# Two graph layers with attention on one core: order of batch 1, of the adjacency transposes, of the folds and of the ending

## The chip, the cores and the metric

The kernel runs on one core of one Trainium2 chip. The metric is the device time of one execution in microseconds (us). The kernel before takes 2221.71 us (median of three runs, 2218.53 to 2224.95). Its profiled execution spans 2219.8 us from the first to the last instruction; all times inside the kernel count from that start. A core has a matrix engine (TensorE, PE in the profile), a vector engine (VectorE, DVE), an activation engine (ScalarE, ACT), GpSimd (POOL) and SyncE (SP), which here issues nearly all transfers (DMA). Each engine takes its instructions in the order in which the program gives them.

## The reference, cut to what matters

Sixteen batches of x (1024 nodes by 256 channels) share one adjacency matrix of 1024 by 1024. Two layers follow each other, each added to its input and normalized over the channels:

```python
# layer 0
c_adj = x.mean(-1)                                  # one mean per node
A = abs(abs(sigmoid(c_adj_i - c_adj_j) - 0.5) - 0.5) * 2
Wg = adj * (A + A.T) * 0.5
q = relu((x.T @ Wg) * para)                         # the query graph, 4 heads of 64
k, v = split(x @ kv_w)
x1 = layernorm(x + softmax(q k.T * scale) v)
# layer 1
h1 = relu(x1 @ w1_loop + adj @ (x1 @ w1_neigh) + b1)
h2 = relu(h1 @ w2_loop + adj @ (h1 @ w2_neigh) + b2)
out = layernorm(x1 + (x1 + h2) * 0.5)
```

## The kernel before

Everything is float32, and a float32 matmul is recorded as two instructions. `run` (line 810) writes the order of all work out by hand; nothing reorders it (`tc.manual_schedule`). The loop over b (line 861) does the attention of batch b in four units of a head pair and half of the nodes (`UNITS`), and lays other batches' work into the gaps between the units: the convolutions of earlier batches, the queries of batch b+1.

`Attention.scores(u)` (line 505) makes eight score tiles of 128 by 1024 in PSUM; ACT exponentiates each into a tile `pr`, and DVE adds the eight up into `acc` (line 522), turns the sum (`accB`, line 524) and reduces it to `den_part` (line 526). `outputs(u)` (line 528) multiplies the `pr` by the values. `add(u)` (line 539) folds `den_part` over partitions with one matmul (line 545), then DVE divides, adds the result to the blocked residual `xB`, and reduces it to `sums` (line 556).

A mean or a variance over 256 channels is taken from a blocked layout with two tiles of 128 channels. DVE reduces each tile to 32 columns (`part` or `sums`, two blocks of columns), and `fold_sums` (line 252) adds the partitions of both with two matmuls into one PSUM tile. There are three such folds for most batches: `means` (line 260) for the query graph of the next batch, `BlockedNorm.mean` (line 305) and `BlockedNorm.variance` (line 319).

The query graph of a batch needs the weighted adjacency, tile by tile: ACT makes the likeness (line 381), DVE multiplies it by a row block of adj (`times_adj`, line 387), PE multiplies (`step`). Batches 0 and 1 use the plain `Queries` (line 364), later ones `FastQueries` (line 407), which saves one product in eight by sums of blocks (`left`, `right`).

The convolutions need adj transposed. After batch 0's attention the branch at line 946 loads adj once more in a blocked layout (`adj_blocked`, line 204) and DVE turns it (`turn_adj`, line 840) into three constant half tiles and two row tiles `rows01`. For later batches the products of two batches are joined with block sums of the adjacency (`Joined`, line 737); these sums are made once, by `adj_sums` (line 189), in batch 1's second gap (`gap1`, line 889, the branch without `both`), and parked in DRAM. That gap also has the first product of batch 0's convolution, `c1.first(rows01)` (line 644), and `weigh_first` (line 881), the first weighted tiles of batch 2's query graph. Each `Joined.run` (line 772) runs seven products in an order of its own and calls other work between them.

SBUF for tiles of 128 by 1024 comes from one pool of 23 buffers (`row_tile`, line 99). A new tile waits until the last reader of the buffer that it gets is done, a DMA to DRAM included.

After the loop, from line 1007 on, the last two batches' convolutions are joined, and batch 15's second half is done alone: `second` (line 676) with 32 matmul records, then `ending` (line 715), which takes the output in four quarters of 256 nodes. Each quarter has its products (`outer`, line 686), its residual (line 692), its statistics (line 273), a power on POOL for the deviation (line 282), and then `leave`, which normalizes on DVE (line 288) and writes. Batch 14's output is normalized on DVE just before (`finish`, line 711).

Of the kernel before, what the change touches and what calls it, by code (L numbers as in the profile page):

```python
# [10 lines left out]
F32 = mybir.dt.float32  # L11
I32 = mybir.dt.int32
AF = mybir.ActivationFunctionType
ALU = mybir.AluOpType
# [4 lines left out]
def kernel(  # L19
# [31 lines left out]
    nc = tc.nc  # L51

    B, N, C = x.shape
    P = 128
    NT = N // P
    NC = C // P
# [5 lines left out]
    TJ = FB // P  # L62
# [8 lines left out]
    NB = N // S  # L71

    LIFT = 32.0
    UNITS = [(pair, j) for pair in range(NC) for j in range(NJ)]
# [5 lines left out]
    small = ctx.enter_context(tc.tile_pool(name="small", bufs=4))  # L80
# [105 lines left out]
    def adj_block(i, j, k, rows01):  # L186
        return of_rows(rows01, k) if (i, j) == (0, 1) else half_adj[i, j][:, k, :]
# [56 lines left out]
    def prepare(blocked, name):  # L244

        xT = channel_major(blocked, f"xT_{name}")
        part = small.tile([P, NC, NB], F32, tag="part", name=f"part_{name}", bufs=2)
        for cc in range(NC):
            nc.vector.tensor_reduce(part[:, cc, :], blocked[cc].rearrange("p (bn r) -> p bn r", r=S), AX.X, ALU.add)
        return xT, part  # L250

    def fold_sums(part, name):

        pm = bank_psum(f"{name}_ps")
        for cc in range(NC):
            nc.tensor.matmul(pm[:, 0:NB], fold.rearrange("p a k -> p (a k)"), part[:, cc, :],
                             start=(cc == 0), stop=(cc == NC - 1))
        return pm[:, 0:NB]

    def means(part, name):  # L260

# [34 lines left out]
    def by_node(t):  # L296
        return t.rearrange("p (bn r) -> p bn r", r=S)

    class BlockedNorm:
# [12 lines left out]
        def squares(self):  # L312
            self.part = small.tile([P, NC, NB], F32, tag="part", name=f"sq_part_{self.name}", bufs=2)
            for cc in range(NC):
                sq = row_tile(f"sq_{self.name}_{cc}")
                nc.scalar.activation(sq, self.xB[cc], AF.Square)  # L316
                nc.vector.tensor_reduce(self.part[:, cc, :], by_node(sq), AX.X, ALU.add)

        def variance(self):
            self.rstd = small.tile([P, NB], F32, tag="rstd1", name=f"rstd1_{self.name}", bufs=2)  # L320
# [171 lines left out]
    class Attention:  # L492
# [46 lines left out]
        def add(self, u):  # L539

            b, (pair, j) = self.b, UNITS[u]
            half = FB // S
            pd = bank_psum(f"den_ps_{b}_{u}")
            den = pd[:, 0:2 * half]
            nc.tensor.matmul(den, fold.rearrange("p a k -> p (a k)"), self.part.pop(u), start=True, stop=True)
            rden = small.tile([P, half], F32, tag="rden", name=f"rden_{b}_{u}", bufs=2)
            for s in range(2):
                rows = slice(s * HD, (s + 1) * HD)
                nc.vector.reciprocal(rden[rows, :], den[rows, ts(s, half)])
            nc.vector.tensor_tensor(den_min, den_min, den, ALU.min)  # L550
            nc.vector.tensor_tensor(den_max, den_max, den, ALU.max)
            o = by_node(self.o.pop(u))
            nc.vector.tensor_mul(o, o, rden.unsqueeze(2).to_broadcast([P, half, S]))
            dst = by_node(self.xB[pair][:, ts(j, FB)])
            nc.vector.tensor_add(dst, dst, o)
            nc.vector.tensor_reduce(self.sums[:, pair, ts(j, half)], dst, AX.X, ALU.add)

    def safe_attention(b, xb, qT, kT, v):

# [54 lines left out]
    class GraphConv:  # L614
# [58 lines left out]
                nc.tensor.transpose(pt[:, ts(i, P)], self.h1T[:, ts(j * TJ + i, P)], ident)  # L673
            nc.scalar.copy(self.h1[:, ts(j, FB)], pt)

        def second(self, rows01):

            self.uT = row_tile(f"uT_{self.b}")
            for j in range(NJ):
                pu = half_psum(f"u_ps_{self.b}_{j}")  # L680
                for mt in range(NT):
                    nc.tensor.matmul(pu, self.h1[:, ts(mt, P)], adj_block(mt // TJ, j, mt % TJ, rows01),  # L682
                                     start=(mt == 0), stop=(mt == NT - 1))
                nc.scalar.copy(self.uT[:, ts(j, FB)], pu)

        def outer(self, g, per, p2):
# [25 lines left out]
            normalize(self.mv, self.rstd, self.x)  # L712
            nc.sync.dma_start(out=dst.rearrange("(t p) c -> p t c", p=P), in_=self.x)

        def ending(self, dst):

            per = FB // C
            parts = []

            def leave(g, mv, rstd):  # L720
                rows = self.x[:, g * per:(g + 1) * per, :]
                normalize(mv, rstd, rows, per)
                nc.sync.dma_start(out=dst[g * per * P:(g + 1) * per * P, :].rearrange("(t p) c -> p t c", p=P), in_=rows)

            for g in range(NT // per):
                p2 = (bank_psum if g % 2 else half_psum)(f"h2e_ps_{g}")
                self.outer(g, per, p2)
                self.residual(g, per, p2)
                mv = small.tile([P, per, 2], F32, tag="mv_e", name=f"mv_e_{g}", bufs=2)
                statistics(mv, self.x[:, g * per:(g + 1) * per, :], range(per), f"e{g}")  # L730
                rstd = reciprocal_deviation(mv, f"e{g}", EPS2, per)
                if parts:
                    leave(*parts.pop())
                parts.append((g, mv, rstd))
            leave(*parts.pop())

    class Joined:
# [34 lines left out]
        def run(self, between=None):  # L772
            c1, c2, b = self.c1, self.c2, self.b
            between = between or {}

            def turn_to(n):
                for f in between.get(n, ()):
                    f()

            first, third, second = (half_psum(f"hu_ps_{b}_{i}") for i in range(3))  # L780
            s12, s34 = (row_tile(f"snap_{b}_{k}") for k in range(2))
            p1, u1, u3, p7 = s12[:, 0:FB], s12[:, FB:N], s34[:, 0:FB], s34[:, FB:N]
            self.product(1, first, start=True)
            nc.scalar.copy(p1, first)
            turn_to(1)
            c1.loop(third, 0, start=True)
            self.product(2, third)
            nc.vector.tensor_add(p1, p1, third)
            turn_to(2)
            self.product(6, first, again=True)  # L790
            nc.scalar.copy(u1, first)
            c1.relu(0, p1)
            turn_to(6)
            self.product(7, second, start=True)
            nc.scalar.copy(p7, second)
            turn_to(7)
            self.product(5, first, again=True)
            nc.scalar.copy(u3, first)
            turn_to(5)
            self.product(4, second, again=True)  # L800
            c2.uT = row_tile(f"uT_{c2.b}")
            nc.vector.tensor_add(c2.uT[:, 0:FB], u1, second)
            nc.gpsimd.tensor_add(c2.uT[:, FB:N], u3, p7)
            turn_to(4)
            c1.loop(first, 1, again=True)
            self.product(3, first, again=True)
            c1.relu(1, first)
            turn_to(3)

    def run():  # L810
# [27 lines left out]
        rows01 = []  # L838
# [22 lines left out]
        for b in range(B):  # L861
# [19 lines left out]
            def weigh_first():  # L881
                q.times_adj(0)
                q.times_adj(TJ)
                q.right(0)

            def next_means():
                q.c_row, q.c_col = means(ready["part"], str(b + 1))

            def gap1():
                for t in (0, TJ):  # L890
                    q.load(t)
                if both:
                    both.fetch(1, 4)
                    both.run({1: (lambda: q.left(nc.gpsimd),),
                              2: (lambda: att.add(1), next_means),
                              6: (lambda: q.likeness(0), lambda: c3 and c3.moments()),
                              7: (lambda: q.likeness(TJ),),
                              5: (weigh_first,),
                              4: (lambda: c3 and c3.finish(out[b - 3]),),
                              3: (c1.turn_blocks,)})  # L900
                else:
                    q.left(nc.gpsimd)
                    next_means()
                    for t in (0, TJ):
                        q.likeness(t)
                    c1.first(rows01)
                    att.add(1)
                    weigh_first()
                    c1.turn_blocks()
                    store("01", rows01)  # L910
                    adj_sums(rows01)

            def gap2():
                if both:
# [31 lines left out]
            if more and not c1:  # L946
# [9 lines left out]
                q.times_adj(4)  # L956
                q.step(1)
                att.add(3)
                turn_adj(range(4))
                for mt in range(4, NT):  # L960
                    tiles[mt] = adj_blocked(mt)
                q.times_adj(5)
# [12 lines left out]
                qT = q.end()  # L975
                norm.scale()
                norm.spread()
                turn_adj(range(4, NT))
                kT, v = keys(b + 1, xT), values(b + 1, xT)
            elif more:  # L980
                xT = ready["xT"]
# [36 lines left out]
        c2.last()  # L1018
        c1.turn(1)
        c2.moments()  # L1020
        c1.second(rows01)
        c2.finish(out[B - 2])
        c1.ending(out[B - 1])

    with tc.manual_schedule():
        run()
# [66 lines left out]
```

## Time and profile before

| engine | busy us | share of the span |
|---|---|---|
| PE | 2183.0 | 98% |
| DVE | 1858.4 | 84% |
| ACT | 965.4 | 43% |
| POOL | 328.5 | 15% |

The table is part 1 of the page. The mean granted TensorE clock is 0.995 of full speed. DMA moves 258.61 MB, a mean of 117 GB/s. A line of the timeline has the start and the time from the first start to the last end of a run of like instructions, the engine, the source line, what is written from what, the number of records, and in brackets the idle time ahead of it with what ended it. In the chain of waits a matmul's time counts only until the next one starts, so that it is shorter than the same matmul in the timeline. Where batches 2 to 14 run, PE has no idle gaps worth the name: batch 2's first scores start at 290.81 and batch 3's at 425.76 us.

### The profile page before, as it was taken

The numbers are of one execution on the slowest core, as the hardware profiler recorded it, in microseconds if no ns is written. First come the engines' busy times: TensorE is split into PE (matmuls) and PEld (weight loads), VectorE is DVE, ScalarE is ACT, GpSimd is POOL, SyncE is SP. The second block draws the span as 40 slices with busy tenths as digits, with TensorE's granted clock in tenths as the row PEclk, the third lists the DMA queues.
The fourth block names the chain that finished last, engine by engine and source line by source line (L and its number), as shares of the span: only waits on it lengthen the run. The fifth ranks groups of instructions, "written<-read, shape, count | busy, mean of one in ns | idle before, by whom it ended". The sixth has DMA issues, their size and how long they took to land.

```text
span 2219.8 us, 22852 instructions
## 1 busy us (share of the span) xinstructions
PE 2183.0 (98%) x8190; PEld 1044.3 (47%) x8190; DVE 1858.4 (84%) x2413; ACT 965.4 (43%) x1056; POOL 328.5 (15%) x177
## 2 busy tenths in 40 slices
PE   8997999999999999999999999999999999999997
PEld 4343354544445444454444444445454544544454
DVE  4987987899888988889889788898889888888965
ACT  4733545443454344544435454434544445444410
POOL 1000030120302103021030210303012020210021
PEclk9999999999999999999999999999999999999999
DMA  8292562452726436363364634637254273633342
GB/s 192 86 138 51 153 180 67 75 172 57 180 86 110 137 60 178 98 150 104 59 176 89 171 95 72 167 65 180 86 89 158 57 180 92 139 113 62 108 144 85
DMA packets 586360, 258.61 MB, mean 117 GB/s; under 512 B 488064, under 2 KB 552448, under 8 KB 586240
## 3 DMA queue, kind: packets, MB, share of 16 engines
q1 hardware_dynamic: 585968, 256.56, 47.8%
q8 instruction: 66, 1.08, 0.2%
q14 instruction: 54, 0.44, 0.1%
q10 hardware_dynamic: 272, 0.52, 0.1%
HBM read 210.90 MB, written 46.14 MB: 116 GB/s over the span
## 4 chain that ended last, share of the span: by engine, by line
PE 90%; DVE 5%; SPq 2%; DMA 1%; POOL 1%; issue 0%; ACT 0%; DVEq 0%; POOLq 0%
PE s L513 19%; PE av L533 18%; PE hu_ps L769 15%; PE g_ps L470 15%; PE k_ps L347 4%; PE v_ps L359 4%; PE h_ps L689 2%; PE h_ps L690 2%; PE t_ps L629 2%; PE hu_ps L636 2%; DVE acc L522 2%; PE g_ps L397 2%; SPq L108 1%; PE u_ps L682 1%; PE h_ps L649 1%; DMA xB<-in_x_dram 1%
## 5 line engine op out<-in xcount | busy, mean ns | idle before, releaser
L516 ACT ACTIVATE pr<-s 128x1024 f32<-128x1024 f32 x512 | 477.0, 1051 | 194.7 <-PE s L513 180.7
L522 DVE TENSOR_TENSOR acc<-acc,pr 128x1024 f32<-128x1024 f32 x384 | 493.2, 1284 | 40.7 <-DVE acc L522 0.5
L513 PE MATMUL s<-qT,kT 64*128 64x512 f32 x2048 | 461.1, 600 | 12.4 <-ACT pr L516 11.7
L533 PE MATMUL av<-pr,v 128*64 128x512 f32 x2048 | 453.6, 595 | 0.0
L513 PEld LDWEIGHTS s<-qT,kT 64*128 64x128 f32 x2048 | 191.9, 187 | 250.3 <-ACT pr L516 127.4
L533 PEld LDWEIGHTS av<-pr,v 128*64 128x64 f32 x2048 | 141.3, 137 | 300.1 <-issue 290.3
L323 POOL TENSOR_TENSOR rstd<-rstd,neg_half 128x32 f32<-128x32 f32 x16 | 87.0, 5441 | 1169.1 <-DVE rstd L321 1169.1
L383 ACT ACTIVATE wg<-c_row,c_col 128x1024 f32<-128x1024 f32 x128 | 147.1, 1149 | 81.9 <-DVE accB L524 49.0
L389 DVE SCALAR_TENSOR_TENSOR wg<-wg,adj 128x1024 f32<-128x1024 f32 x128 | 149.7, 1209 | 10.7 <-ACT wg L384 10.7
L769 PE MATMUL hu_ps<-adj,R 128*128 128x512 f32 x360 | 158.4, 596 | 0.0
L384 ACT ACTIVATE wg<-wg 128x1024 f32<-128x1024 f32 x128 | 135.4, 1058 | 4.1
L316 ACT ACTIVATE sq<-xB_a 128x1024 f32<-128x1024 f32 x32 | 33.8, 1057 | 196.3 <-DVE xB_a L310 182.8
L347 PE MATMUL k_ps<-xT,kvw_sb 128*128 128x512 f32 x256 | 117.1, 601 | 0.0
L470 PE MATMUL g_ps<-wg,S 128*128 128x512 f32 x224 | 116.7, 603 | 0.0
L470 PE MATMUL g_ps<-T,S 128*128 128x512 f32 x224 | 114.4, 592 | 0.0
L359 PE MATMUL v_ps<-kvw_sb,xT 128*128 128x256 f32 x512 | 113.1, 379 | 0.0
L769 PE MATMUL hu_ps<-adjT,t 128*128 128x512 f32 x240 | 109.5, 599 | 2.2 <-ACT t L632 2.2
L328 DVE TENSOR_TENSOR xB_a<-xB_a,rstd 128x1024 f32<-128x1024 f32 x32 | 38.8, 1254 | 84.4 <-POOL rstd L323 84.4
L470 PE MATMUL g_ps<-wg,x 128*128 128x512 f32 x224 | 109.0, 599 | 0.0
L520 DVE TENSOR_TENSOR acc<-pr,pr 128x1024 f32<-128x1024 f32 x64 | 78.0, 1218 | 34.6 <-ACT pr L516 34.6
L359 PEld LDWEIGHTS v_ps<-kvw_sb,xT 128*128 128x128 f32 x512 | 97.3, 190 | 20.0 <-issue 7.7
L769 PEld LDWEIGHTS hu_ps<-adj,R 128*128 128x128 f32 x360 | 67.3, 190 | 78.9 <-issue 78.0
(162 smaller groups left out, 2727.3 us busy)
## 6 DMA issues: line engine op xcount, KB each, us to landing
adj<-in_adj_dram SPq DMA_DIRECT2D x128, 512.0 KB, 4.5
adj<-adjT SPq DMA_DIRECT2D x120, 512.0 KB, 8.2
xB_a<-in_x_dram SPq DMA_DIRECT2D x128, 128.0 KB, 4.1
x1d<-xB_a SPq DMA_DIRECT2D x128, 128.0 KB, 3.4
x<-x1d SPq DMA_DIRECT2D x16, 1024.0 KB, 6.6
xB<-in_x_dram SPq DMA_DIRECT2D x120, 128.0 KB, 4.6
x<-in_x_dram SPq DMA_DIRECT2D x15, 1024.0 KB, 7.2
out_dram<-x SPq DMA_DIRECT2D x15, 1024.0 KB, 4.6
```

Source lines behind the costliest of these rows:

```text
L323: nc.gpsimd.tensor_tensor(self.rstd, self.rstd, neg_half, ALU.pow)
L347: nc.tensor.matmul(pk[:, ts(j, FB)], kvw_sb[:, cc, ts(kb, P)], xT[:, cc, ts(j, FB)], start=(cc == 0), stop=(cc == NC - 1))
L359: nc.tensor.matmul(pv[:, ts(i, C)], xT[:, cc, ts(g * per + i, P)], kvw_sb[:, cc, C:2 * C], start=(cc == 0), stop=(cc == NC - 1))
L383: nc.scalar.activation(wg, self.c_row, AF.Abs, bias=self.c_col[:, t:t + 1], scale=-1.0)
L384: nc.scalar.activation(wg, wg, AF.Tanh, scale=-0.5)
L389: nc.vector.scalar_tensor_tensor(wg, wg, 1.0, self.adj.pop(t), op0=ALU.add, op1=ALU.mult)
L470: nc.tensor.matmul(self.p[n], x_n[:, k, :], w_n, start=(k == 0), stop=(k == TJ - 1))
L513: nc.tensor.matmul(ps[:, ts(s, FB)], self.kT[rows, pair, ts(mt, P)], self.qT[rows, pair, ts(j, FB)], start=True, stop=True)
L516: nc.scalar.activation(pr, ps, AF.Exp)
L522: nc.vector.tensor_add(acc, acc, pr)
L533: nc.tensor.matmul(pav[s * HD:(s + 1) * HD, :], self.v[:, mt, pair * P + s * HD:pair * P + (s + 1) * HD], self.pr[mt][:, ts(s, FB)], start ...
L769: nc.tensor.matmul(dst, self.x[n][:, k, :], half_adj[w][:, k, :] if w else of_rows(rows, k), start=(start and k == 0), stop=(k == TJ - 1), ...
```

## The change

The change has five parts. (1) In batch 1's second gap, the adding of unit 1, the likeness tiles, the block sums of the adjacency and the first weighted tiles come ahead of batch 0's first convolution product instead of behind it. (2) The first eight transposes of the adjacency, which lay inside batch 0's query-graph steps for batch 1, go behind it, so that all sixteen follow each other. (3) DVE joins the two column blocks of a partial sum with one addition of 128 by 32, so that a fold has one matmul instead of two. (4) In `Joined.run` the loop product (`c1.loop`) comes ahead of product 1 instead of between products 1 and 2. (5) At the end, the quarters 0 and 1 are done inside batch 15's second product, as soon as their half is ready, and batch 14's last normalization goes from DVE to ACT, in the form scale times x plus a shift. The purpose is fewer waits and fewer instructions on TensorE and a shorter end behind its last matmul.

```diff
@@ -247,15 +247,17 @@
         part = small.tile([P, NC, NB], F32, tag="part", name=f"part_{name}", bufs=2)
         for cc in range(NC):
             nc.vector.tensor_reduce(part[:, cc, :], blocked[cc].rearrange("p (bn r) -> p bn r", r=S), AX.X, ALU.add)
+        join(part)
         return xT, part
 
     def fold_sums(part, name):
 
         pm = bank_psum(f"{name}_ps")
-        for cc in range(NC):
-            nc.tensor.matmul(pm[:, 0:NB], fold.rearrange("p a k -> p (a k)"), part[:, cc, :],
-                             start=(cc == 0), stop=(cc == NC - 1))
+        nc.tensor.matmul(pm[:, 0:NB], fold.rearrange("p a k -> p (a k)"), part[:, 0, :], start=True, stop=True)
         return pm[:, 0:NB]
+
+    def join(part):
+        nc.vector.tensor_add(part[:, 0, :], part[:, 0, :], part[:, 1, :])
 
     def means(part, name):
 
@@ -315,6 +317,7 @@
                 sq = row_tile(f"sq_{self.name}_{cc}")
                 nc.scalar.activation(sq, self.xB[cc], AF.Square)
                 nc.vector.tensor_reduce(self.part[:, cc, :], by_node(sq), AX.X, ALU.add)
+            join(self.part)
 
         def variance(self):
             self.rstd = small.tile([P, NB], F32, tag="rstd1", name=f"rstd1_{self.name}", bufs=2)
@@ -554,6 +557,8 @@
             dst = by_node(self.xB[pair][:, ts(j, FB)])
             nc.vector.tensor_add(dst, dst, o)
             nc.vector.tensor_reduce(self.sums[:, pair, ts(j, half)], dst, AX.X, ALU.add)
+            if u == len(UNITS) - 1:
+                join(self.sums)
 
     def safe_attention(b, xb, qT, kT, v):
 
@@ -673,14 +678,20 @@
                 nc.tensor.transpose(pt[:, ts(i, P)], self.h1T[:, ts(j * TJ + i, P)], ident)
             nc.scalar.copy(self.h1[:, ts(j, FB)], pt)
 
-        def second(self, rows01):
+        def neighbours(self, j, pu, mts, rows01):
+            for mt in mts:
+                nc.tensor.matmul(pu, self.h1[:, ts(mt, P)], adj_block(mt // TJ, j, mt % TJ, rows01),
+                                 start=(mt == 0), stop=(mt == NT - 1))
+
+        def second(self, rows01, between=None):
 
             self.uT = row_tile(f"uT_{self.b}")
             for j in range(NJ):
                 pu = half_psum(f"u_ps_{self.b}_{j}")
-                for mt in range(NT):
-                    nc.tensor.matmul(pu, self.h1[:, ts(mt, P)], adj_block(mt // TJ, j, mt % TJ, rows01),
-                                     start=(mt == 0), stop=(mt == NT - 1))
+                self.neighbours(j, pu, range(TJ), rows01)
+                if j and between:
+                    between()
+                self.neighbours(j, pu, range(TJ, NT), rows01)
                 nc.scalar.copy(self.uT[:, ts(j, FB)], pu)
 
         def outer(self, g, per, p2):
@@ -712,7 +723,16 @@
             normalize(self.mv, self.rstd, self.x)
             nc.sync.dma_start(out=dst.rearrange("(t p) c -> p t c", p=P), in_=self.x)
 
-        def ending(self, dst):
+        def finish_aside(self, dst):
+
+            shift = small.tile([P, NT], F32, tag="shift", name=f"shift_{self.b}", bufs=1)
+            nc.vector.scalar_tensor_tensor(shift, self.mv[:, :, 0], -1.0, self.rstd, op0=ALU.mult, op1=ALU.mult)
+            for t in range(NT):
+                nc.scalar.activation(self.x[:, t, :], self.x[:, t, :], AF.Identity, bias=shift[:, t:t + 1],
+                                     scale=self.rstd[:, t:t + 1])
+            nc.sync.dma_start(out=dst.rearrange("(t p) c -> p t c", p=P), in_=self.x)
+
+        def ending(self, dst, rows01, aside):
 
             per = FB // C
             parts = []
@@ -722,7 +742,7 @@
                 normalize(mv, rstd, rows, per)
                 nc.sync.dma_start(out=dst[g * per * P:(g + 1) * per * P, :].rearrange("(t p) c -> p t c", p=P), in_=rows)
 
-            for g in range(NT // per):
+            def quarter(g):
                 p2 = (bank_psum if g % 2 else half_psum)(f"h2e_ps_{g}")
                 self.outer(g, per, p2)
                 self.residual(g, per, p2)
@@ -732,6 +752,10 @@
                 if parts:
                     leave(*parts.pop())
                 parts.append((g, mv, rstd))
+
+            self.second(rows01, lambda: (aside(), quarter(0), quarter(1)))
+            quarter(2)
+            quarter(3)
             leave(*parts.pop())
 
     class Joined:
@@ -780,10 +804,10 @@
             first, third, second = (half_psum(f"hu_ps_{b}_{i}") for i in range(3))
             s12, s34 = (row_tile(f"snap_{b}_{k}") for k in range(2))
             p1, u1, u3, p7 = s12[:, 0:FB], s12[:, FB:N], s34[:, 0:FB], s34[:, FB:N]
+            c1.loop(third, 0, start=True)
             self.product(1, first, start=True)
             nc.scalar.copy(p1, first)
             turn_to(1)
-            c1.loop(third, 0, start=True)
             self.product(2, third)
             nc.vector.tensor_add(p1, p1, third)
             turn_to(2)
@@ -901,14 +925,14 @@
                 else:
                     q.left(nc.gpsimd)
                     next_means()
+                    att.add(1)
                     for t in (0, TJ):
                         q.likeness(t)
-                    c1.first(rows01)
-                    att.add(1)
-                    weigh_first()
-                    c1.turn_blocks()
                     store("01", rows01)
                     adj_sums(rows01)
+                    weigh_first()
+                    c1.first(rows01)
+                    c1.turn_blocks()
 
             def gap2():
                 if both:
@@ -956,7 +980,6 @@
                 q.times_adj(4)
                 q.step(1)
                 att.add(3)
-                turn_adj(range(4))
                 for mt in range(4, NT):
                     tiles[mt] = adj_blocked(mt)
                 q.times_adj(5)
@@ -975,7 +998,7 @@
                 qT = q.end()
                 norm.scale()
                 norm.spread()
-                turn_adj(range(4, NT))
+                turn_adj(range(NT))
                 kT, v = keys(b + 1, xT), values(b + 1, xT)
             elif more:
                 xT = ready["xT"]
@@ -1018,9 +1041,7 @@
         c2.last()
         c1.turn(1)
         c2.moments()
-        c1.second(rows01)
-        c2.finish(out[B - 2])
-        c1.ending(out[B - 1])
+        c1.ending(out[B - 1], rows01, lambda: c2.finish_aside(out[B - 2]))
 
     with tc.manual_schedule():
         run()
```

## The prediction

> **What bounds the kernel now.** I read the page's part 1 first, then the waits of PE, then the timelines of PE and DVE around the longest of these waits, then the chain of waits in a quiet batch, and last the DVE timeline of the end.
>
> ```profile
> PE 2183.0 (98%) x8190; PEld 1044.3 (47%) x8190; DVE 1858.4 (84%) x2413; ACT 965.4 (43%) x1056; POOL 328.5 (15%) x177
> PE s L513 <- ACT pr L516: 11.7, 2, 10.1
> ...
> PE hu_ps L769 <- ACT t L632: 2.2, 2, 1.1
> PE den_ps L545 <- DVE den_part L526: 1.9, 1, 1.9
> PE g_ps L397 <- DVE wg L389: 1.8, 1, 1.8
> ```
>
> PE has work in 98% of the span and follows itself almost everywhere. So an instruction taken off PE shortens the kernel by its own time, and besides that only the waits (us in total, times, longest) and the work behind the last matmul can be won. DVE, 84% busy, matters where it makes PE wait. That is batch 1; here is PE's timeline:
>
> ```profile
> 187.60 0.63 PE L256 MATMUL mean_ps<-part,fold 128*128 128x32 f32 x4
> ...
> 205.31 0.30 PE L545 MATMUL den_ps<-den_part,fold 128*128 128x32 f32 x2
> 205.55 3.70 PE L513 MATMUL s<-qT,kT 64*128 64x512 f32 x16
> 210.84 1.13 PE L513 MATMUL s<-qT,kT 64*128 64x512 f32 x4 [1.59 <-ACT pr L516]
> 222.08 4.58 PE L513 MATMUL s<-qT,kT 64*128 64x512 f32 x12 [10.11 <-ACT pr L516]
> 226.58 7.09 PE L533 MATMUL av<-pr,v 128*64 128x512 f32 x32
> 235.62 0.46 PE L545 MATMUL den_ps<-den_part,fold 128*128 128x32 f32 x2 [1.95 <-DVE den_part L526]
> 236.01 8.73 PE L513 MATMUL s<-qT,kT 64*128 64x512 f32 x32
> ```
>
> and DVE's over the same gap:
>
> ```profile
> 194.73 0.19 DVE L270 TENSOR_REDUCE c_col<-own 128x8 f32<-128x32 f32 x1
> 205.66 0.52 DVE L549 RECIPROCAL rden<-den_ps 64x16 f32<-64x16 f32 x2 [10.73 <-PE den_ps L545]
> ```
>
> DVE sits idle for 10.73 us because unit 1's fold stands on PE behind the whole convolution product. Then it works without a gap until 235.6, and PE waits in its turn.
>
> A fold's price stands in the chain of waits of batch 3's query graph (start, us, what):
>
> ```profile
> 396.35 0.14 PE den_ps L545 x2
> ...
> 402.58 0.36 PE sum_ps L256 x4
> ```
>
> One matmul takes 0.14 us and two take 0.36, so the second is worth 0.22. At the end DVE runs alone (its timeline):
>
> ```profile
> 2201.68 0.69 DVE L694 TENSOR_TENSOR z<-h2e_ps,b_sb 128x512 f32<-128x512 f32 x1 [4.47 <-PE h2e_ps L690]
> ...
> 2204.41 0.69 DVE L694 TENSOR_TENSOR z<-h2e_ps,b_sb 128x512 f32<-128x512 f32 x1
> ...
> 2211.16 0.68 DVE L694 TENSOR_TENSOR z<-h2e_ps,b_sb 128x512 f32<-128x512 f32 x1
> ...
> 2214.88 0.73 DVE L288 TENSOR_SCALAR x<-x,mv_e,rstd_e 128x256 f32<-128x256 f32 x2 [0.27 <-POOL rstd_e L282]
> ```
>
> Four quarters follow each other, 2.73 us each up to the next z, plus 0.73 for a quarter's normalization.
>
> [...] in the windows view the granted clock is 0.50 from 218 to 222, inside the 10.11 us gap, and 0.50 again from 236 to 238, behind a gap of only 1.95; behind gaps of 1.10 and 1.81 it stays 1.00. [...] the page shows one load, at the start. [...]
>
> **The change part by part.**
>
> *Folds.* Batches 1 to 15 have three folds, batch 0 two: 47. One lies in batch 1's stalled stretch and is counted there, so 46 x 0.22 = 10.1 us come off PE. The joins add 47 small DVE additions; min on 128x32 (L550) takes 0.19 us and starts 0.10 before the next instruction, so I take 0.1 us each. A join lies ahead of its fold, so I looked at the slack in batch 3: the last `sums` are done at 400.6 and the fold comes at 402.4; `sq_part` is done at 410.4, its fold comes at 414.9. Behind the join on DVE stands `pair(3)`; its first part ends at 402.8 for a matmul at 405.4. Slack of 1.8 us and more covers 0.1 to 0.2, so the joins cost nothing. Bounds: 8 to 10.5.
>
> *Transposes.* Eight transposes (3.67 + 1.31 us with a DMA wait, 124.14 to 129.4) go from ahead of `times_adj(5)` to the end. PE's 1.81 us wait was for that multiplication, which now ends near 125.4, ahead of its matmul at 128.5: 1.8 us won. The sixteen then take 16 x 0.6 = 9.7 us. The scale must wait for POOL's power (5.45 us, L323), whose variance comes 2 us earlier; scale and spread end near 146.4, the transposes at 156.2. Batch 1's first addition of `acc` is due at 158.66 - 2.2 = 156.4. It just fits; a miss is taken up by the 2.60 us for which DVE waits next (L549 at 173.62). Bounds: 1 to 2.
>
> *Batch 1.* PE now has unit 1's fold right behind the mean's, at 188.1, but `den_part` is done by DVE only at 192.65. That is a new wait of 4.6 us, and behind it on PE stand the 17.2 us of the convolution and all of unit 2. DVE: c_col done at 194.9, the adding 2.8, eight block sums 9.3 (214.55 to 223.84), weights 4.9 (208.46 to 213.38), h1B 1.15: free at 213.1. PE: 192.9 + 17.2 = 210.1, or 211.8 with a clock dip [...]. I take the dip, since 4.6 us is longer than a gap that showed one. Scores start at 211.8; the first addition of `acc` comes 3.15 us later (as from 425.76 to 428.91 in batch 3), at 214.95; DVE takes 11.7 us for eight tiles and their reduction (223.84 to 235.58): `den_part` is done at 226.7. PE's outputs end at 211.8 + 7.07 + 7.02 = 225.9, so 0.8 of the wait of 1.95 is left. Unit 3's scores take 7.07 at full clock and end at 234.0 instead of 244.67: 10.7 us won. Without the dip it is 12.2. The buffers: ACT's `pr` waited for h1B's store (10.2 us by ACT's waits) since 18 buffers were taken in between; now the sums are written from 197.7 to 207.0 and their stores (1.25 us apart before, each landing in 5.6) start earlier, so they should be free when the first `pr` asks at 212. Bounds: 7.5 to 12.5.
>
> *Loop product first.* In the gaps of the loop PE is busy either way: nothing. In the two runs of the end, PE waits 1.10 us each for t's copy; 1.72 us of loop products now cover it: 2.2 us.
>
> *End.* Quarters 0 and 1 (3.46 us of PE) move ahead of the last 16 matmul records, so the product ends at 2199.91 + 3.46 = 2203.37. Quarter 2 needs the copy that ACT then makes (0.58 and some hand-over: 0.65), a new wait on PE with only the last two quarters behind it. Its products end at 2205.8; DVE: 2.73 + 0.73 + 2.73 + 0.73, then the power (0.72) in part behind it: the last normalization starts at 2212.85 instead of 2214.88. 2.0 us won. [...] Bounds: 0.5 to 2.5.
>
> Sum: 10.1 + 1.8 + 10.7 + 2.2 + 2.0 = 26.8. 2221.7 - 26.8 = 2194.9.
>
> **The rivals.**
>
> *The wait moves (0.24).* PE's new 4.6 us, a clock dip [...] and late buffers leave 7.5 in batch 1; the joins push some folds (8.5); the end gives 0.5, the rest 3. 19.5 us: 2202. For it: the dip behind only 1.95 us. Against it: DVE, which sets unit 2's end, has no other idle time to gain or lose there.
>
> *No dip at all (0.14).* 12.2 in batch 1 and the upper bounds (10.5, 2, 2.2, 2.5): 29.4 us, 2192.3. For it: the gap is one of DVE's order, and 1.81 us left the clock alone. [...]
>
> *DVE becomes the bound (0.03), slower.* If each join waited in line and `sums` reached PE late by 2 us in all 16 batches, 32 us would be lost against 26.8 won: about 2227. Against it: the slack of 1.8 us and DVE's 361 us of idle time. I also leave 0.02 for folds and waits that only just cancel.
>
> **How the numbers follow.** The forecast as worked out has 0.57, and its time is 2194.9. The range takes in the first rival and the second, with the spread of a measurement of about 3 us on the lower side of the estimate: 2188 to 2203. Faster by more than 0.3% means below 2215: 0.95; within it 0.02; slower 0.03.
>
> **What would show it.** Right: L256 with 94 records instead of 188; PE's waits for `pr` and for t gone; one of about 4.6 us for `den_part` near 186 in their place; no wait for wg at L389; batches 0.66 us closer (134.95 to 134.3); the last L288 ending about 10 us behind the last product of L682 instead of 15.7. Wrong: a wait for `sums` or `part` at L256 in every batch, DVE late for batch 1's `acc`, or ACT held by buffers under unit 2.

## The result, and the profile after

The changed kernel takes 2200.87 us (median, 2200.6 to 2201.87) against 2221.61 for the kernel before: a ratio of 0.9907, 95% interval 0.989 to 0.9924. 20.7 us are won where 26.8 were forecast. The time lies inside the forecast's range; 6 us are missing.

Part 1 of the changed kernel's page, busy time and instructions of each engine:

```profile
PE 2172.8 (99%) x8096; PEld 1032.4 (47%) x8096; DVE 1864.0 (85%) x2453; ACT 969.3 (44%) x1064; POOL 328.1 (15%) x177
```

PE is still the engine that is nearly always busy. Its waits in the changed kernel (us in total, times, longest):

```profile
PE den_ps L548 <- DVE o L540: 5.6, 1, 5.6
...
PE k_ps L350 <- DVE U L483: 2.8, 13, 0.5
PE den_ps L548 <- DVE den_part L529: 0.8, 1, 0.8
...
PE h2e_ps L700 <- ACT uT L695: 0.7, 1, 0.7
```

The waits for `pr`, for t and for wg are gone, as forecast. The wait of 5.6 for unit 1's fold and of 0.7 for the copy at the end are the two that the forecast named. The line with U was not forecast: in 13 of the 14 query graphs of batches 2 to 15, the keys (the matmuls into `k_ps`) now wait for the DVE addition U (L483), the first of the additions that end a query graph.

Batch 1, PE's timeline:

```profile
184.31 0.41 PE L256 MATMUL mean_ps<-part,fold 128*128 128x32 f32 x2
190.28 0.64 PE L548 MATMUL den_ps<-den_part,fold 128*128 128x32 f32 x2 [5.56 <-DVE o L540]
190.73 3.74 PE L641 MATMUL h_ps<-x1T,w1l_sb 128*128 128x512 f32 x4
...
209.84 7.14 PE L516 MATMUL s<-qT,kT 64*128 64x512 f32 x32
216.91 7.09 PE L536 MATMUL av<-pr,v 128*64 128x512 f32 x32
224.78 0.41 PE L548 MATMUL den_ps<-den_part,fold 128*128 128x32 f32 x2 [0.78 <-DVE den_part L529]
225.12 7.14 PE L516 MATMUL s<-qT,kT 64*128 64x512 f32 x32
```

The four records of the loop product behind the wait take 3.74 us, in the kernel before 1.96:

```profile
188.06 1.96 PE L636 MATMUL h_ps<-x1T,w1l_sb 128*128 128x512 f32 x4
```

That is the clock dip of the forecast: in the windows view the granted clock is 0.50 from 187.5 to 194.3. Unit 2 has no gap inside any more.

The end, DVE's timeline, first lines of quarters 0, 2 and 3 and the last normalization:

```profile
2178.71 0.69 DVE L705 TENSOR_TENSOR z<-h2e_ps,b_sb 128x512 f32<-128x512 f32 x1 [3.54 <-PE h2e_ps L701]
...
2186.54 0.69 DVE L705 TENSOR_TENSOR z<-h2e_ps,b_sb 128x512 f32<-128x512 f32 x1 [1.55 <-PE h2e_ps L701]
...
2189.92 0.69 DVE L705 TENSOR_TENSOR z<-h2e_ps,b_sb 128x512 f32<-128x512 f32 x1
...
2193.65 0.74 DVE L290 TENSOR_SCALAR x<-x,mv_e,rstd_e 128x256 f32<-128x256 f32 x2 [0.26 <-POOL rstd_e L284]
```

Only two quarters are left behind the last product.

To see where the time went, I cut the span of each profiled execution at five matmuls that all kernels have. "Periods" is the sum of the 13 intervals from batch 2's first keys to batch 15's.

| stage, us | before | after | won |
|---|---|---|---|
| start to batch 1's first keys | 141.65 | 138.36 | 3.29 |
| to batch 2's first keys | 134.84 | 125.71 | 9.13 |
| the 13 periods | 1756.25 | 1752.35 | 3.90 |
| to batch 15's first `t_ps` | 71.67 | 71.55 | 0.12 |
| to batch 15's second product (first `u_ps`) | 81.60 | 78.51 | 3.09 |
| to the end | 33.79 | 32.32 | 1.47 |

13 periods with three folds of 0.22 each should have given 8.6 us; they gave 3.9. The second row was forecast at 11.1 (10.7 and two folds) and gave 9.1. These two rows hold the missing 6 us. The chain of waits at batch 3's keys shows why; here it is in the changed kernel (start, us, what):

```profile
395.56 2.37 DVE sq_part L319 x2
397.92 0.02 issue
397.95 0.19 DVE sq_part L260
398.14 0.61 DVE U L483
398.75 0.04 issue
398.79 3.70 PE k_ps L350 x8
402.49 0.14 PE sum_ps L256 x2
```

The fold is down to 0.14, but the chain now runs through DVE: squares, join, U, and then PE. `k_ps` takes the PSUM tile whose second half U reads last. Here are U, PE's last query-graph matmuls and the keys, from the timelines of both kernels. Under them is a line of the waits of each for PEld, the loading of a matmul's weights, which the profile lists apart from PE. Before:

```profile
410.35 0.68 DVE L480 TENSOR_TENSOR U<-P,g_ps 128x512 f32<-128x512 f32 x1
410.59 1.02 PE L470 MATMUL g_ps<-wg,S 128*128 128x512 f32 x2
411.44 3.60 PE L347 MATMUL k_ps<-xT,kvw_sb 128*128 128x512 f32 x8
...
PEld k_ps L347 <- DVE U L480: 4.5, 13, 0.6
```

After:

```profile
398.06 0.68 DVE L483 TENSOR_TENSOR U<-P,g_ps 128x512 f32<-128x512 f32 x1
397.60 1.02 PE L473 MATMUL g_ps<-wg,S 128*128 128x512 f32 x2
398.79 3.70 PE L350 MATMUL k_ps<-xT,kvw_sb 128*128 128x512 f32 x8 [0.17 <-DVE U L483]
...
PEld k_ps L350 <- DVE U L483: 14.5, 14, 1.3
```

Before, U ended at 411.03 and the keys started at 411.44, 0.85 us behind the start of the last query-graph matmuls. After, U ends at 398.74; the keys start 0.05 behind that and 1.19 behind those matmuls. So they are 0.34 us late, and the eight records take 0.10 longer. This 0.44 is more than the bracket's 0.17: the wait is counted from the listed end of the matmul ahead, and before, the keys started 0.17 ahead of that end.

### The profile page after: what moved, and what is told of

It reads as the page before. It is cut to its first block, busy times and chain, and to the rows that moved or that the text cites. A ratio compares the mean times of both kernels' runs of the same rounds, so it can differ in the third digit from the quotient of the medians.

```text
span 2198.8 us, 22720 instructions
## 1 busy us (share of the span) xinstructions
PE 2172.8 (99%) x8096; PEld 1032.4 (47%) x8096; DVE 1864.0 (85%) x2453; ACT 969.3 (44%) x1064; POOL 328.1 (15%) x177
## 4 chain that ended last, share of the span: by engine, by line
PE 72%; DVE 24%; issue 2%; ACT 1%; DMA 0%; DVEq 0%; SPq 0%; POOLq 0%; ACTq 0%; POOL 0%
PE hu_ps L793 16%; PE s L516 15%; PE av L536 15%; DVE acc L525 6%; PE k_ps L350 5%; PE v_ps L362 5%; PE t_ps L634 3%; PE h_ps L700 2%; PE hu_ps L641 2%; PE g_ps L400 2%; PE h_ps L701 2%; DVE wg L392 2%; DVE sq_part L319 1%; DVE wg L446 1%; DVE T L445 1%
```

## The experiments

All medians are of several timed runs; the kernel before took 2221.4 to 2222.0 beside them. The changed kernel was not timed again beside them, so differences from it of less than about 1 us say little.

**Folds alone.** The kernel before with `join` and the single matmul in `fold_sums`, nothing else:

```diff
+        nc.tensor.matmul(pm[:, 0:NB], fold.rearrange("p a k -> p (a k)"), part[:, 0, :], start=True, stop=True)
-        for cc in range(NC):
-            nc.tensor.matmul(... part[:, cc, :], start=(cc == 0), stop=(cc == NC - 1))
+    join(part) / join(self.part) / join(self.sums)
```

> Only the joined sums and single folds are put into the kernel before. Theory A (in every query graph of batches 2 to 15 the keys' first PSUM buffer is now awaited from the DVE addition U, because DVE is 0.23 us later by two joins and PE 0.44 us earlier by two folds, against a slack of 0.41): each of 14 batches keeps only 0.23 of its 0.66 us, so 47 x 0.22 - 14 x 0.43 = 4.3 us are won, about 2217.3. Theory B (the folds pay in full and the gain is lost elsewhere): 10.3 us won, about 2211.3.

Measured 2216.81 (2214.21 to 2218.93), ratio 0.9976, interval 0.9968 to 0.9983: 5.2 us won. Its trace has the same wait:

```profile
PE k_ps L350 <- DVE U L483: 2.4, 13, 0.5
```

So half of the folds' gain is lost with a wait that this part alone brings. That is near theory A's 4.3 us and far from theory B's 10.3. The sizes in theory A do not give its own result, though: 0.23 later and 0.44 earlier against a slack of 0.41 make 0.26 a batch, and its 0.43 was read from the periods. The true sizes come with the idle joins below.

**Two matmuls for a fold again, no joins.** The reverse of it, in the changed kernel:

```diff
-        nc.tensor.matmul(... part[:, 0, :], start=True, stop=True)
+        for cc in range(NC):
+            nc.tensor.matmul(... part[:, cc, :], start=(cc == 0), stop=(cc == NC - 1))
-        join(part) / join(self.part) / join(self.sums)
```

> The changed kernel with two matmuls for each fold again and no joins. Theory A: only 4 to 5 us are lost, about 2205.4, and the keys' wait for U is gone. Theory B: 10 us are lost, about 2211.

Measured 2205.58 (2204.37 to 2209.28): 4.7 us lost, and no wait of PE for U in the trace. Theory A again. About the same amount from both sides says that this part hardly depends on the others.

**Joins on POOL.**

```diff
-        nc.vector.tensor_add(part[:, 0, :], part[:, 0, :], part[:, 1, :])
+        nc.gpsimd.tensor_add(part[:, 0, :], part[:, 0, :], part[:, 1, :])
```

> The changed kernel with the joins on POOL instead of DVE. Theory A: DVE reaches U 0.23 us sooner in each batch, the wait for U falls from about 0.34 to 0.1 us, and 14 x 0.23 = 3 us are won: about 2197.7. Theory C (DVE's additions do not matter, PE is merely early): no change, 2200.9. If POOL's join comes late for its fold, PE waits at the fold instead and the time is above 2200.9.

Measured 2200.28 (2199.02 to 2202.5): by the total, no change, which was theory C's number. The trace, of the longest of the four executions, says otherwise. PE's wait for U is gone, where theory A left 0.1; most periods are 134.3 to 134.5 instead of 134.72, and the 13 together 1748.8 instead of 1752.4: 3.5 us were won there, theory A's 3 and a little more. They were lost again ahead of that: 1.0 before batch 1's keys, where PE waits 0.6 once for POOL's join at a fold, and 4.4 in batch 1, where the block differences `q.left` on POOL, queued behind the join, now fall into unit 1's additions. DVE's timeline of these additions, first here and then in the changed kernel:

```profile
179.95 11.61 DVE L525 TENSOR_TENSOR acc<-acc,pr 128x1024 f32<-128x1024 f32 x6
```

```profile
179.19 7.87 DVE L525 TENSOR_TENSOR acc<-acc,pr 128x1024 f32<-128x1024 f32 x6
```

DVE needs 3.7 us more while POOL works from 179.92 to 187.8 (its last three operations take 2.14 to 2.25 us each, in the changed kernel, where they come earlier, 1.27), and the wait for unit 1's fold grows from 5.6 to 9.1. That both were slow together is measured; why was not tested.

**U ahead of the squares.** `q.end` is split, and its first copy and addition come ahead of the two reductions:

```diff
-                q.step(2, lambda: (norm.mean(), norm.squares()))
+                q.step(2, norm.mean)
                 q.step(3)
+                q.head()          # copy of p1 on ACT, U = p1 + p6 on DVE
+                norm.squares()
                 qT = q.end()
```

> The changed kernel with the addition U (and the copy it needs) given to DVE ahead of the two reductions of the squares. Theory A: U is done about 2.3 us sooner, the keys never wait, and up to 14 x 0.43 = 6 us are won: about 2195. Theory B and C: the wait named in the trace is not what limits PE, no change, 2200.9.

Measured 2195.0 (2194.52 to 2195.74), ratio 0.9882, interval 0.9867 to 0.9897. DVE at the same place, from its timeline:

```profile
394.65 0.68 DVE L479 TENSOR_TENSOR U<-P,g_ps 128x512 f32<-128x512 f32 x1
395.25 2.33 DVE L319 TENSOR_REDUCE sq_part<-sq 128x32 f32<-128x1024 f32 x2
397.62 0.19 DVE L260 TENSOR_TENSOR sq_part<-sq_part 128x32 f32<-128x32 f32 x1
```

U is done at 395.33, and the keys start at 397.69. PE and PEld no longer wait for U anywhere. Six of the 13 periods are 134.28, which is 134.95 less 0.67: the three folds in full; the others are up to 0.4 longer. The 13 periods take 1747.5, 8.7 us less than before, where the folds' arithmetic says 8.6. The same instructions in another order give what the forecast had promised for the folds. U first with two matmuls for a fold was not run; the periods leave no room for a gain of its own.

**Joins that nobody reads.** Two matmuls for a fold, and DVE writes the joined sums to a spare tile:

```diff
+        nc.vector.tensor_add(spare, part[:, 0, :], part[:, 1, :])
```

> The changed kernel with two matmuls for each fold and with the joins done by DVE into a spare tile that nobody reads: DVE's cost of the joins without PE's gain. Theory A (a slack of 0.41 us at U, of which the joins take 0.23): no wait at the keys, the same 2205.6 as with two folds and no joins. Theory F (the joins alone make the wait): 14 x 0.2 = 3 us more, about 2208.5.

Measured 2209.71 (2208.19 to 2210.23), 4.1 us above the kernel with two matmuls and no joins. Theory A's number falls, theory F's is near. Most periods are about 135.17 instead of 134.95, 3 us in all; the rest is spread. U, the last query-graph matmuls and the keys of batch 3 show that the joins alone use up the slack at U:

```profile
400.23 0.68 DVE L489 TENSOR_TENSOR U<-P,g_ps 128x512 f32<-128x512 f32 x1
400.00 1.02 PE L479 MATMUL g_ps<-wg,S 128*128 128x512 f32 x2
400.96 3.70 PE L356 MATMUL k_ps<-xT,kvw_sb 128*128 128x512 f32 x8
```

The keys start 0.05 behind U's end (0.05 or 0.06 in all 14 batches of this trace). That is 0.1 us late, and the eight records take 0.1 more: the 0.2 that the periods show. PE's waits list only two of the 14.

A join is larger than I took it. In batch 3 of the changed kernel (DVE's timeline):

```profile
387.17 0.69 DVE L559 TENSOR_REDUCE sums<-xB_a 128x16 f32<-128x512 f32 x1
387.89 0.19 DVE L260 TENSOR_TENSOR sums<-sums 128x32 f32<-128x32 f32 x1
388.00 2.35 DVE L392 SCALAR_TENSOR_TENSOR wg<-wg,adj 128x1024 f32<-128x1024 f32 x2
```

From the reduction's start to the next multiplication it is 0.83 us with the join; in the kernel before it is 0.60 (399.93 to 400.53). The join starts only when the reduction that it reads has ended (387.86), while the multiplication behind it starts 0.08 before the join's end. The join costs 0.23, and that of the squares 0.22 (2.50 from 395.56 to 398.06, 2.28 before). Two of them make 0.45. U ended 0.41 ahead of the keys, and 0.05 of that is the least distance seen here, so the slack was 0.36.

**Batch 1's gap as before.** The old order in the changed kernel:

```diff
-                    att.add(1)
                     for t in (0, TJ):
                         q.likeness(t)
-                    store("01", rows01)
-                    adj_sums(rows01)
-                    weigh_first()
                     c1.first(rows01)
+                    att.add(1)
+                    weigh_first()
                     c1.turn_blocks()
+                    store("01", rows01)
+                    adj_sums(rows01)
```

> The changed kernel with batch 1's second gap in the order of before. Theory of the prediction: about 9 to 10.7 us are lost (9.2 by the two traces, from unit 0's scores to unit 3's), 2210 to 2211.6, and the waits of 10.1 and 1.95 us in unit 2 come back. Rival (the wait only moved): at most 5 us lost, 2206.

Measured 2208.95 (2207.73 to 2211.68): 8.1 us lost, with PE's wait of 10.25 us for `pr` back. The interval between batch 1's and batch 2's keys is 133.38 instead of 125.71, 7.7 more. That is below the 9 that I expected from the two traces, because in this kernel the scores behind the wait for unit 2's fold ran at full clock: 7.14 us, not 8.73 as in the kernel before. The waits were 2.03 and 1.95 us; of two such gaps one brought a dip and one didn't. What decides that was not tested.

**The fold between the halves of the product.** PE no longer waits for unit 1's fold:

```diff
-                    att.add(1)
...
+                    c1.first(rows01, (0,))
+                    att.add(1)
                     store("01", rows01)
                     adj_sums(rows01)
                     weigh_first()
-                    c1.first(rows01)
+                    c1.first(rows01, (1,))
```

> The changed kernel with unit 1's fold between the two halves of the convolution product instead of ahead of both, so that PE does not wait 5.6 us for it. Theory D (DVE, which has 2.8 us of idle time in this stretch, sets the end of unit 2): the wait only moves to unit 2's fold, and between 0 and 1.7 us are won, 2199.2 to 2200.9. Rival E (PE's wait and the clock dip behind it are lost time): 5.6 + 1.7 us won, about 2193.6.

Measured 2202.12 (2201.54 to 2203.48), if anything slower than the changed kernel (by 1.3 us). PE's timeline:

```profile
193.71 0.30 PE L548 MATMUL den_ps<-den_part,fold 128*128 128x32 f32 x2
...
209.67 7.09 PE L536 MATMUL av<-pr,v 128*64 128x512 f32 x32
224.01 0.64 PE L548 MATMUL den_ps<-den_part,fold 128*128 128x32 f32 x2 [7.25 <-DVE den_part L529]
224.57 9.54 PE L516 MATMUL s<-qT,kT 64*128 64x512 f32 x32
```

PE reaches unit 2's fold 7 us sooner and then waits 7.25 us for DVE; unit 2's fold comes at 224.0 instead of 224.8. The scores behind it take 9.54 us instead of 7.14, so the clock dip, too, only moved, and grew. Rival E falls: the 5.6 us were no lost time, since DVE sets the end of unit 2. Theory D had the place right and the dip too small.

**The block sums first, with U first.** Beside the edit of U above:

```diff
-                    att.add(1)
...
                     store("01", rows01)
                     adj_sums(rows01)
+                    c1.first(rows01, (0,))
+                    att.add(1)
                     weigh_first()
-                    c1.first(rows01)
+                    c1.first(rows01, (1,))
```

> The changed kernel with U ahead of the squares (2195.0 measured alone) and, in batch 1's gap, with the block sums of the adjacency first on DVE, then unit 1's adding, whose fold stands between the halves of the convolution product. Theory D: DVE's 2.8 us of idle time go, 1.6 to 3.3 us are won, 2191.7 to 2193.4. Rival E: PE has no wait for unit 1's fold left, 7 us won, 2188.

Measured 2195.76 (2194.81 to 2196.18): no better than 2195.0. Batch 1's interval falls from 125.11 to 124.06 us, so a little of DVE's idle time was won, but PE still waits 5.46 us for unit 2's denominators, with a dip behind it (8.59 us for the scores instead of 7.14), and the 13 periods happened to take 1.7 us more. Rival E fails again; theory D's 1.6 to 3.3 us were too many.

**Half of the block sums elsewhere.** The order of the last experiment, but DVE makes the second half of the sums while it would wait for POOL's power at the end of batch 1:

```diff
-                    adj_sums(rows01)
+                    adj_sums(rows01, (0,))
...
                 kT = keys(b + 1, xT, norm.variance)
+                if b == 1:
+                    adj_sums(rows01, (1,))
                 norm.scale()
```

> The changed kernel with U ahead of the squares, unit 1's fold between the halves of the convolution product, and half of the block sums of the adjacency taken out of batch 1's gap to DVE's wait of 5.55 us for the deviation at the end of batch 1. Theory D (DVE's work sets the end of unit 2): unit 2's denominators are done 4.65 + 2.8 us sooner, PE meets them without a long wait or a clock dip, and about 7 us are won over 2195.0: 2188. Rival (PE's own order sets it): no more than 2 us won, 2193.

Measured 2189.54 (2188.17 to 2195.82), ratio 0.9855, interval 0.984 to 0.987. Batch 1's interval is 117.73 us, 7.4 less than with U first alone. PE's timeline, and DVE's at the end of batch 1:

```profile
217.22 0.41 PE L550 MATMUL den_ps<-den_part,fold 128*128 128x32 f32 x2 [0.81 <-DVE den_part L531]
217.55 7.14 PE L518 MATMUL s<-qT,kT 64*128 64x512 f32 x32
```

```profile
266.36 1.23 DVE L200 TENSOR_TENSOR adjT<-adjT,adjT 128x1024 f32<-128x1024 f32 x1
269.33 2.36 DVE L331 TENSOR_TENSOR xB_a<-xB_a,rstd 128x1024 f32<-128x1024 f32 x2 [1.75 <-POOL rstd L326]
```

DVE still waits 1.75 us for POOL after the sums, so they were free there. Theory D's account holds: PE meets unit 2's fold without a long wait or a dip. By the medians 5.5 us were won over 2195.0, where it said 7. The profiled execution was the longest of the four; there, batches 2 and 7 took 138 us instead of 134.3. In batch 2 DVE waited 2.35 us for the next batch's blocked input; whether the later stores of the sums brought that on was not tested. This version beats both kernels: 32 us under the kernel before, 11 under the change.

**The transposes back.** The first eight of the adjacency transposes (four tiles, two each) inside batch 0's query-graph steps again:

```diff
                 att.add(3)
+                turn_adj(range(4))
...
-                turn_adj(range(NT))
+                turn_adj(range(4, NT))
```

> The changed kernel with the first eight transposes of the adjacency back inside the query graph. The prediction: 1.8 us lost, about 2202.7, and PE's wait of 1.8 us for wg is back. Rival (the late transposes cost as much at batch 1's first sum): no change, 2200.9.

Measured 2205.19 (2204.02 to 2207.07): 4.3 us lost. Batch 1's keys start at 140.56 instead of 138.36, 2.2 later, behind a wait of 2.03 for wg; the other 2 us are spread over batch 1 and the 13 periods (0.5 and 1.4), where the part has no work. The sum of the 13 periods differs by as much between runs whose edits leave them alone (1752.4 in the changed kernel, 1753.2 to 1754.8 with the gap, the fold or the end moved), so 2.2 is what can be put down to it. The start spreads a little too: batch 1's keys come at 138.0 to 139.0 in the runs that leave it as in the changed kernel.

**The loop product back, and the end back.** Two kernels:

```diff
-            c1.loop(third, 0, start=True)
             self.product(1, first, start=True)
             ...
+            c1.loop(third, 0, start=True)
             self.product(2, third)
```

```diff
-            self.second(rows01, lambda: (aside(), quarter(0), quarter(1)))
-            quarter(2)
-            quarter(3)
+            self.second(rows01)
+            aside()
+            for g in range(NT // per):
+                quarter(g)
...
-        c1.ending(out[B - 1], rows01, lambda: c2.finish_aside(out[B - 2]))
+        c1.ending(out[B - 1], rows01, lambda: c2.finish(out[B - 2]))
```

> The changed kernel with the loop product back between products 1 and 2. The prediction: 2.2 us lost, about 2203.1, with two waits of 1.1 us for t's copy back. By the two traces it may be up to 2.5.

> The changed kernel with batch 15's second product whole ahead of all four quarters and batch 14's last normalization on DVE, as before. The prediction: 2.0 us lost; by the two traces 1.7: 2202.6 to 2202.9. Rival (the wait for the copy takes back what the earlier quarters win): no change.

Measured 2204.59 (2204.0 to 2206.28) and 2203.4 (2202.15 to 2204.79): 3.7 and 2.5 us lost. With the loop product back, PE's two waits of 1.1 us for t are back too. By their stages, from `t_ps` to `u_ps` 81.15 instead of 78.51 us, 2.6 more, and from `u_ps` to the end 34.12 instead of 32.32, 1.8 more; the rest is again scatter in stages that the edit doesn't touch.

## Why the prediction was right or wrong

The direction, the range and every named wait came true. So did two other signs: L256 has 94 matmul records, and the last normalization ends 10.6 us behind the last product. One sign did not: the batches came 0.23 us closer and not 0.66. By its steps:

- **Folds, 10.1 forecast, 4.7 to 5.2 measured.** This is the step that failed. The price of the second matmul (0.22) was right: with U first, the 13 periods give 8.7 where 13 x 0.66 is 8.6. Wrong was "so the joins cost nothing". I had compared the joins with the slack at their own folds and at one matmul of step 3, and not at what stands behind them on DVE: U, whose end frees the keys' PSUM tile. The profile of before had it: U ended 0.41 us ahead of the keys in batch 3, and the waits of before name U for the keys' weights 13 times (4.5 us). The joins were also sized at 0.1 us where each cost 0.22 or 0.23. Against the point where the keys could have started (0.85 behind the last query-graph matmuls), U ended 0.41 ahead before, 0.06 behind with the idle joins and 0.29 behind in the changed kernel: 0.47 from the joins and 0.23, about one fold, from PE being earlier. Each batch lost 0.34 in the wait and 0.10 behind it. The periods say the same: 0.66 less the 0.23 that they gained is 0.43. 14 x 0.43 is 6.0 us, and U first won 5.9 back. That this is also the whole shortfall is chance: batch 1 was short by about 1.6 us more, and the other stages and the scatter of the periods gave about as much. The slower rival had the mechanism, but looked for it at the folds.
- **Transposes, 1.8.** 2.2 by the stage, 4.3 by the totals. The late transposes ended at 155.0 and the first `acc` started at 155.37 after 0.36 of idle time: "it just fits" held.
- **Batch 1, 10.7.** 8.1 by undoing it, 7.7 by that kernel's interval, in which one dip of 1.6 was missing; 9.1, folds included, by the interval before and after. The new wait was 5.56, not 4.6: PE was 3.3 us earlier and DVE's `den_part` 3.05, and the fold waited for the PSUM bank that DVE frees with `o` (190.23), 0.6 behind `den_part`. The clock dip cost 1.8 us, where the forecast's step from 210.1 to 211.8 has 1.7, my estimate. The kernel before shows as much behind its gap of 1.95 us: a granted clock of 0.50 for 3.4 us (235.84 to 239.25, windows view), half of which is 1.7. How long a gap has to be for a dip was not shown. DVE's sum was right to 0.1 (from the scores' start 3.15 to `acc`, then 11.7), and so was the rest of the wait, 0.78 for 0.8. No `pr` waited for a buffer.
- **Loop product, 2.2.** 2.6 by the stage. A wait of 1.10 cost 1.3, somewhat more than its idle time.
- **End, 2.0.** 1.8 by the stage of the kernel with the end back, 1.5 by that of the kernel before. The wait for the copy was 0.68 for 0.65, and ACT's eight normalizations took 4.04 us (0.58 to 0.60 us each). They ended 4.62 us ahead of the copy at 2183.87, so they were hidden. The changed kernel, too, has one table load, at 1.24 (1.28 us).

Of the rivals, "the wait moves" had the nearest time (2202), but mostly for another reason than its own: no buffer was late, the dip cost about what the forecast had, and most of the loss lay in the 13 periods.

## What to carry to other kernels

An instruction added on an engine that isn't the bound has to be followed along its queue to the next thing that the bound waits for, PSUM tiles to be freed included; the slack there counts (0.36 us at U, where two joins took 0.45), not the slack at its own consumer (1.8 us and more). Here the waits of the weight loads named that place (4.5 us in the kernel before) when no matmul waited there. A small instruction that reads the result just made can cost more than its own time to the next start: here 0.23 us, not 0.1. Where PE waited and DVE worked almost without a gap, moving PE's instructions only moved the wait (5.56 us at unit 1's fold became 7.25 at unit 2's); taking DVE's work to a place where DVE idled (a wait of 5.56 us for POOL) took most of it away (5.46 us at unit 2's fold became 0.81).

## What the runs showed of the hardware that I had not expected

- A dependent DVE addition of 128 by 32 behind a reduction lengthened the queue by 0.23 us, against 0.11 from its start to the start of the next instruction.
- DVE's six additions of 128 by 1024 took 11.61 us instead of 7.87 while POOL did the block differences.
- Behind a gap on PE of 5.56 us the matmuls took 1.8 us longer (3.74 for 1.96, at a granted clock of 0.50), behind one of 5.46 1.5 (8.59 for 7.14), behind one of 7.25 2.4 (9.54), behind one of 1.95 1.6 (8.73, at 0.50 for 3.4 us) and behind one of 2.03 nothing (7.14). The length of the gap alone does not tell the cost.
- The eight records of key matmuls that start 0.05 us behind the DVE addition whose PSUM tile they take need 3.70 us, without the wait 3.60.
